# Four graph layers in one kernel: small weights as planned steps, and less of the second group's layer 0 ahead of a branch

## The chip, the cores and the metric

The kernel runs on one core of one Trainium2 chip. The metric is device time in microseconds (us), the median over runs of the whole program.

## The reference

The input is `x`, 128 graphs of 128 nodes with 128 features in float32, and `adj`, an integer matrix 128x128 for each graph (here ones and zeros, one in sixteen set). Four layers follow one another, each as `x = x + layer(relu(layernorm(x)))`, here cut to what matters:

```python
# layer 0: relation r = 1..7, masks of adj == r, averaged over neighbours
for r in range(1, 8):
    mask = (adj == r)
    agg += (mask / clip(mask.sum(2), 1e-6)) @ h @ rel_weights[r]
out = relu(layernorm(agg + h @ self_w.T + self_b) * ln_gamma + ln_beta)
# layer 1: every pair of nodes, a batch norm over all pairs of all graphs
D = abs(h[:, :, None, :] - h[:, None, :, :])           # pairs
p = D @ W1.T + b1
p = leaky((p - mean(p)) / sqrt(var(p) + eps) * g1 + be1)   # mean over batch and pairs
A = softmax(where(adj > 0, p @ W2.T + b2, NEG))
y = leaky(batchnorm(A @ h @ Wg.T + bg))
out = concat([h, y], 2) @ Wt.T + bt
# layer 2: graph attention with 4 heads; layer 3: with one head, elu at the end
```

## The kernel before, in words

The 128 graphs are worked on in 32 groups of four (`G`, `NG`). The program has three long stages. The first does layer 0 and the pair products of layer 1 with their statistics; the second reads the products back, applies the batch norm and the softmax of layer 1; the third does layers 2 and 3. This case concerns the beginning of the first.

**The search and the branch.** Relations 2 to 7 are rare, so the kernel first looks whether `adj` has any entry above 1. `part(c)` loads one of 16 pieces of `adj` (512 KB each, `PARTS`) and `highest(c)` reduces it, on DVE for an even `c` and on ACT for an odd one. `flagged` puts the answer into `flag`. A branch (`tc.If`, L646) reads it on every engine. If relations above 1 occur, a general path computes their share for each group and writes it to `AGG[g]` in DRAM. If not, as here, the other path only writes `selfb`, the broadcast bias, into the whole of `AGG` (L695, two transfers out of the tensors `rest`).

**Layer 0 of a group.** `chain(g)` makes the steps of one group: `load` (x and adj, L428 and L429), `agg` (read of `AGG[g]`, L432), the layer norm's moments on DVE (`mv`) and roots on POOL (`rs`), the mask and the degree, the normed `hn` on ACT, transposes, the products `ph` and `po` on PE, then the second half: `o` (sum with agg, L489), its moments `mvo` and roots `rso`, `oc`, `on`, `end`, the store of x (`x`, L535), the moments and roots for layer 1 (`mvx`, `rsx`) and `h1`, layer 1's input, in two halves. The first `AHEAD` groups are done ahead of the branch with `selfb` in place of `agg`; when the general path is taken, it does them again. Before, `AHEAD` is 2, so groups 0 and 1 are done whole ahead of the branch, and group 2 is only loaded.

**Layer 1's pairs.** For each graph there are four tiles of pairs (`NT`). `difference` (d, L312) subtracts, on DVE for even tiles and on POOL for odd ones; `absolute` is on ACT (L360); `products` on PE (hp, L322 and L325) into two PSUM buffers; `evacuate` copies the product on ACT to a `z` tile of SBUF (L336), one of ten in a ring on the right side of the memory (`held_z`, `FETCHED`); `statistics` is on DVE (L350, L351); and `kept` stores two tiles at a time to DRAM (L343, steps `out0` and `out`). The ring's pool is opened after the branch; the pools of the search and of the branch were closed by then.

**Order.** Each of these is a step with an engine, an estimated cost, the steps that it waits for, and a rank. `_ordered` walks through time, takes at each point the earliest step that can start (the lowest rank among equals), and so writes one program order; each engine executes its steps in that order. There are two such plans, one ahead of the branch and one after it. The plan's costs never touch the hardware: they only set the order. A step on SP is taken to land 3.0 us after its issue (`LANDING`).

**Small weights.** 30 small transfers on SP's queue (biases, norms and weight matrices that later stages use) are written at the head of the second plan, outside of it (`col`, `load`, L198 and L205, and L751 to L766). On the chip 18 of them were issued ahead of the branch and 12 after it, as the trace shows.

Of the kernel before, what the change touches and what calls it, by code (L numbers as in the profile page):

```python
# [9 lines left out]
F32 = mybir.dt.float32  # L10
I32 = mybir.dt.int32
# [6 lines left out]
P = 128  # L18
# [11 lines left out]
ROW = P + 2 * KH  # L30
ON_POOL = {1, 3}
BY_MAX = 0
AHEAD = 2
PARTS = 16
FETCHED = 10
NT = KH // KC
KEPT = 5
# [1 line left out]

ONE, TWO = 4, 2  # L40
PERIOD, FIRST, HOP, LANDING = 12, 5, 0.2, 3.0
HOP1 = 0.4
TINY = 2.0 ** -100
BUFS = {"y": 6, "x": 12, "off": 10, "st": 8, "mv2": 3, "rs2": 3, "nb2": 3, "h": 7, "hT2": 3, "v2": 3, "wr2": 7,
# [4 lines left out]
def _bcast(src, n):  # L49

    return bass.AP(tensor=src.tensor, offset=src.offset, ap=[[0, P], [1, n]])
# [63 lines left out]
def _ordered(steps, limits, hop):  # L115

    named = {s[0]: s for s in steps}
    free, done = dict.fromkeys(("SP", "Pool", "ACT", "DVE", "PE"), 0.0), {}  # L120
    left = {tag: [0.0] * n for tag, n in limits.items()}
    waits = {s[0]: [a for a in s[3] if a in named] for s in steps}
    followers, ready = {}, {e: {} for e in free}
    for name, after in waits.items():
        for a in after:
            followers.setdefault(a, []).append(name)
    missing = {name: len(after) for name, after in waits.items()}

    def released(name):
        engine = named[name][1]  # L130
        ready[engine][name] = max([0.0] + [done[a] + hop * (named[a][1] != engine) for a in waits[name]])

    for name, n in missing.items():
        if n == 0:
            released(name)
    plan = []
    while len(plan) < len(steps):
        best = None
        for engine, names in ready.items():
            could = []  # L140
            for name, since in names.items():
                takes = named[name][4]
                if all(left[tag] for tag in takes):
                    could.append((max([free[engine], since] + [min(left[tag]) for tag in takes]),
                                  named[name][6], name))
            if could:
                first = min(could)[0]
                one = min((c for c in could if c[0] == first), key=lambda c: c[1])
                if best is None or first < best[0]:
                    best = one  # L150
        start, _, name = best
        _, engine, cost, _, takes, gives, _, work = named[name]
        del ready[engine][name]
        free[engine] = start + cost
        done[name] = start + cost + (LANDING if engine == "SP" else 0)
        for tag in takes:
            left[tag].remove(min(left[tag]))
        for tag in gives:
            left[tag].append(start + cost + hop)
        plan.append(work)  # L160
        for f in followers.get(name, ()):
            missing[f] -= 1
            if missing[f] == 0:
                released(f)
    return plan
# [3 lines left out]
def tile_gnn_stack(ctx: ExitStack, tc: tile.TileContext, a: dict, out: bass.AP):  # L169
    nc = tc.nc  # L170
    NB = a["x"].shape[0]
    NG = NB // G

    const = ctx.enter_context(tc.tile_pool(name="const", bufs=1))
# [21 lines left out]
    def load(name, shape, src, pool=const):  # L196
        t = pool.tile(shape, F32, name=name)
        nc.sync.dma_start(t, src)  # L198
        return t

    def col(name, src, n=P, pool=const):

        t = pool.tile([P, 1], F32, name=name)
        for k in range(P // n):
            nc.sync.dma_start(t[k * n:(k + 1) * n, :], src)  # L205
        return t
# [55 lines left out]
    with tc.tile_pool(name="c0", bufs=1) as c0, tc.tile_pool(name="p0", bufs=2) as p0, ExitStack() as ctx0:  # L262
# [2 lines left out]

        sizes = (6, NG - 8)
        rest = [dr.tile([P, n, G, P], F32, tag=f"a{i}", name=f"a{i}") for i, n in enumerate(sizes)]
        AGG = [t[:, i, :, :] for t, n in zip(rest, sizes) for i in range(n)]  # L270
        AGG = [None] * AHEAD + AGG
# [22 lines left out]
        steps = []  # L294

        def step(name, engine, cost, after, rank, work, takes=(), gives=()):
            steps.append((name, engine, cost, after, takes, gives, rank, work))
# [113 lines left out]
        def chain(g, agg=None, again=None):  # L411

            bs = slice(g * G, g * G + G)
            s0 = G * NT * g - 31
            t = {}
            own = lambda *names: [(name, g) for name in names]

            def tile0(name, dtype=F32, **kw):
                pool, tag = p0, name
                if again is not None:  # L420

                    pool, tag = again, {"mask": "mask4", "maskT": "adjT", "o": "adjf"}.get(name, name)
                    kw = dict(bufs=2) if name == "hn" else {}
                t[name] = pool.tile([P, G, P], dtype, tag=tag, name=name, **kw)
                return t[name]

            def loaded():
                nc.sync.dma_start(tile0("x"), a["x"][bs].rearrange("b t c -> t b c"))  # L428
                nc.sync.dma_start(tile0("adj", I32), a["adj"][bs].rearrange("b t s -> t b s"))  # L429

            def added():
                nc.sync.dma_start(tile0("agg"), AGG[g])  # L432
# [66 lines left out]
            def h1(half):  # L499
                if g not in H1:  # L500
                    H1[g] = p0.tile([P, G, P], F32, name="h1", bufs=3)
                for k in (2 * half, 2 * half + 1):
                    nc.scalar.activation(H1[g][:, k, :], t["x"][:, k, :], AF.Relu, bias=t["nb"][:, k:k + 1],  # L503
                                         scale=t["rs"][:, k:k + 1])

            step(("load", g), "SP", 1.2, [("h1", g - 2, 1), ("x", g - 2), ("xp", 2 * g - 5)]
                 + [("part", PARTS - 1)] * (g >= AHEAD), s0 - 2, loaded)
            if agg is None:
                step(("agg", g), "SP", 0.4, own("load"), s0 + 6, added)
            else:  # L510
# [32 lines left out]
        search = ctx0.enter_context(tc.tile_pool(name="sc", bufs=1))  # L543
        found, n_part = {}, P * P // PARTS
# [23 lines left out]
            nc.scalar.copy(selfb, over_group(found["pr"][:, 0, :]))  # L568

        def part(c):  # L570
            found[c] = search.tile([P, n_part], I32, name="part", bufs=PARTS // 2)
            nc.sync.dma_start(found[c], flat[c])

        def highest(c):

            one, by_sum = found.pop(c), c % 2
            if by_sum:
                nc.scalar.activation(one, one, AF.Relu, bias=less_1, accum_out=tops[:, 1, c // 2:c // 2 + 1])
            else:
                nc.vector.tensor_reduce(tops[:, 0, c // 2:c // 2 + 1], one, AX.X, OP.max)  # L580
# [41 lines left out]
        step("on_all", "PE", 0.6, ["small", ("pt", 0)], -98, on_all, takes=("sm",))  # L622
        step("selfb", "ACT", 0.6, ["on_all"], -98, in_group, gives=("sm",))
        for c in range(PARTS):
            step(("part", c), "SP", 20.0 / PARTS, [("top", c - PARTS // 2)], 1 + c / PARTS,
                 lambda c=c: part(c))
            step(("top", c), "ACT" if c % 2 else "DVE", 1.25, [("part", c)], -99, lambda c=c: highest(c))
        step("top", "DVE", 0.4, [("top", c) for c in range(PARTS)], -99, highest_of_all)
        step("ptop", "PE", 0.3, ["top"], -99, one_row, takes=("sm",))
        step("flag", "DVE", 0.4, ["ptop"], -99, flagged, gives=("sm",))  # L630
# [3 lines left out]
        for g in range(AHEAD):  # L634
            chain(g, selfb)

        held = len(steps)
        chain(AHEAD)
        steps[held:], held = steps[held:held + 1], steps[held + 1:]
        with tc.manual_schedule():  # L640
            for work in _ordered(steps, {"sm": 2}, HOP1):
                work()
# [3 lines left out]
        with tc.If(nc.values_load(flag, min_val=0, max_val=1) > 0) as cmp, \  # L646
# [6 lines left out]
            for g in range(NG):  # L653
                x = pr.tile([P, G, P], F32, name="x")
                nc.sync.dma_start(x, a["x"][g * G:g * G + G].rearrange("b t c -> t b c"))
                adj = pr.tile([P, G, P], I32, name="adj")
# [3 lines left out]
                hT = pr.tile([P, G, P], F32, name="hT")  # L660
# [5 lines left out]
                for k in range(G):  # L666
                    mask = pr.tile([P, 6, P], F32, name="mask")
# [56 lines left out]
        a2 = const.tile([P, 2, 4], F32, name="a2")  # L724
        nc.gpsimd.memset(a2, 0.0)

        steps += held[1:]
        held[0][-1]()
        for g in range(NG):
            for half in range(2):  # L730
                features(g, half)
            if g > AHEAD:
                chain(g)
        for i in range(NT * NB):
            pairs(i)
        step("fetch", "SP", 0.8, [("hs", NT * NB - 2), ("st", NT * NB - 2 * NT), ("out", NB - G - 1)], NT * NB, first_fetches)
        with tc.manual_schedule():

            b1 = col("b1", a["b1"], 64)
            g1 = col("g1", a["g1"], 64)  # L740
            be1 = col("be1", a["be1"], 64)
            wgT = load("wgT", [P, P], a["WgT"])
            bg = col("bg", a["bg"])
            gg = col("gg", a["gg"])
            beg = col("beg", a["beg"])
            wtxT = load("wtxT", [P, P], a["WtT"][0:P])
            bt = load("bt", [P, P], _bcast(a["bt"], P))

            nc.sync.dma_start(w2z[0:64, 31:32], a["W2"])  # L751
            nc.sync.dma_start(w2z[64:128, 32:33], a["W2"])
            b2 = load("b2", [P, 1], bass.AP(tensor=a["b2"].tensor, offset=a["b2"].offset, ap=[[0, P], [1, 1]]))
            w2x = const.tile([P, P + 8], F32, name="w2x")
            nc.sync.dma_start(w2x[:, 0:P], a["W_2"])
            w3x = const.tile([P, P + 2], F32, name="w3x")
            nc.sync.dma_start(w3x[:, 0:P], a["W_3"])
            b_2 = load("b_2", [P, P], _bcast(a["b_2"], P))
            b_2c = col("b_2c", a["b_2"])
            wtyT = load("wtyT", [P, P], a["WtT"][P:2 * P])  # L760
            a3 = const.tile([P, 2, 1], F32, name="a3")
            for part in range(2):
                for hd in range(4):

                    nc.sync.dma_start(a2[32 * hd:32 * hd + 32, part, hd:hd + 1], a["a_2"][32 * (1 - part):][0:32])
                nc.sync.dma_start(a3[:, part, :], a["a_3"][P * (1 - part):][0:P])  # L766

            for work in _ordered(steps, {"sm": 2}, HOP1):
                work()

# [854 lines left out]
```

## Time and profile before

| | us |
|---|---|
| time before, median of 3 runs | 2777.38 (2776.46 to 2777.83) |
| the profiled execution, its own time | 2781.11 |
| its span | 2779.3 |
| busy over the span: DVE, PE, ACT, POOL | 2472.0, 2457.4, 2388.7, 1724.0 |
| first to last copy of a product (L336) | 70.9 to 1524.5 |
| copies number 16, 128, 192, 256 (from 0) begin at | 123.4, 442.9, 625.4, 807.9 |

The span is that of the profiled execution from its first to its last instruction. A time in a view counts from the span's start. In a list of instructions the columns are start, duration, engine and line, operation, output and inputs, count, and in brackets the idle time just ahead with the event that ended it. "SPq" is SP's own queue: there a duration is the time that issuing takes, not the transfer.

### The profile page before, as it was taken

What the parts mean: (1) busy time and instruction counts of PE and PEld (TensorE: products, weight loads), DVE (VectorE), ACT (ScalarE), POOL (GpSimd) and SP (SyncE); (2) the same over time, 40 slices, a digit from 0 to 9 for tenths busy, and PEclk for the clock granted to TensorE, in tenths of its full rate; (3) what the DMA queues carried; (4) which work ended last, traced back from release to release, by engine and by line L of the source; (5) the groups of instructions that cost most, each with busy time, mean ns of one, the idle gap of its engine ahead of it and who ended that gap; (6) DMA issues with size and microseconds to landing.
All of it is one profiled execution on the core that took longest, in us unless ns stands there. A gap on an engine that the chain in (4) does not pass through costs nothing.

```text
span 2779.3 us, 42065 instructions
## 1 busy us (share of the span) xinstructions
PE 2457.4 (88%) x14521; PEld 1182.0 (43%) x14521; DVE 2472.0 (89%) x4712; ACT 2388.7 (86%) x2837; POOL 1724.0 (62%) x1629
## 2 busy tenths in 40 slices
PE   3899999999999999999998789888888897999896
PEld 2333333333333333333332344444444445777675
DVE  4899999999999999999999688888888887899976
ACT  4899999999999999999998778778778766899985
POOL 5799999999999999999997001111000115565642
PEclk7999999999999999999999899999999999999998
DMA  7455555555555555555543899999999971121110
GB/s 283 171 223 201 212 201 210 210 212 201 208 201 208 211 209 207 208 207 215 206 193 125 330 409 411 410 411 410 409 410 410 409 266 54 46 69 58 58 31 25
DMA packets 195933, 635.66 MB, mean 229 GB/s; under 512 B 32755, under 2 KB 100470, under 8 KB 132214
## 3 DMA queue, kind: packets, MB, share of 16 engines
q1 hardware_dynamic: 195264, 632.62, 58.6%
q8 instruction: 120, 1.97, 0.3%
q14 instruction: 111, 0.91, 0.1%
q10 hardware_dynamic: 438, 0.17, 0.0%
HBM read 328.84 MB, written 303.89 MB: 228 GB/s over the span
## 4 chain that ended last, share of the span: by engine, by line
ACT 33%; PE 22%; DVE 19%; issue 11%; DMA 10%; POOL 3%; SPq 1%; ACTq 0%; DVEq 0%; POOLq 0%
ACT d L360 11%; ACT z L336 11%; PE hp L322 6%; PE ps L871 5%; DMA rows<-sk 4%; DVE d L312 3%; DMA u<-rows 3%; DVE z L914 3%; DMA z<-hp 3%; PE hp L325 2%; ACT h L1229 2%; PE pk L878 2%; PE pv L1345 2%; ACT o L462 1%; ACT h L503 1%
## 5 line engine op out<-in xcount | busy, mean ns | idle before, releaser
L312 POOL TENSOR_TENSOR d<-xe 128x2048 f32<-128x2048 f32 x256 | 1074.1, 4202 | 67.1 <-PE hp L322 48.9
L322 PE MATMUL hp<-d,w1T 128*64 128x512 f32 x4096 | 999.4, 603 | 119.8 <-ACT z L336 96.8
L360 ACT ACTIVATE d<-d 128x2048 f32<-128x2048 f32 x384 | 734.6, 1935 | 24.7 <-POOL d L312 18.2
L312 DVE TENSOR_TENSOR d<-xe,xp 128x2048 f32<-128x2048 f32 x256 | 579.5, 2264 | 5.8 <-PE hp L322 3.1
L322 PEld LDWEIGHTS hp<-d,w1T 128*64 128x64 f32 x4096 | 286.2, 137 | 640.4 <-issue 466.6
L336 ACT COPY z<-hp 128x1024 f32<-128x1024 f32 x512 | 516.9, 1028 | 47.1 <-PE hp L325 24.4
L962 POOL TENSOR_TENSOR x<-x,bt 128x512 f32<-128x512 f32 x32 | 46.5, 1455 | 672.1 <-DMA x<-x 629.0
L350 DVE BATCH_NORM_STATS2 st<-z 128x6 f32<-128x512 f32 x512 | 349.3, 682 | 42.4 <-ACT z L336 42.1
L351 DVE BATCH_NORM_STATS2 st<-z 128x6 f32<-128x512 f32 (+1 forms) x512 | 329.3, 643 | 0.0
L914 DVE SCALAR_TENSOR_TENSOR z<-z 128x2048 f32<-128x2048 f32 x128 | 296.6, 2317 | 6.5 <-ACT z L896 6.5
L896 ACT ACTIVATE z<-z,bias,scale 128x2048 f32<-128x2048 f32 x128 | 267.1, 2087 | 9.3 <-DVE bias L809 7.7
L325 PE MATMUL hp<-both_t,xw 128*64 128x512 f32 x1024 | 268.3, 596 | 0.0
L900 ACT ACTIVATE zr<-z,bias,scale 128x2048 f32<-128x2048 f32 x128 | 267.3, 2088 | 0.9 <-DMA z<-hp 0.9
L871 PE MATMUL ps<-z,w2z 128*32 128x512 f32 x1024 | 144.7, 638 | 65.1 <-DVE z L914 64.9
L878 PEld LDWEIGHTS pk<-pick,su 128*128 128x128 f32 x1024 | 127.4, 196 | 136.2 <-DVE su L892 94.0
L878 PE MATMUL pk<-pick,su 128*128 128x16 f32 x1024 | 139.9, 269 | 19.9 <-DVE su L892 19.3
L1345 PE MATMUL pv<-wr,e 128*128 128x128 f32 x1024 | 141.7, 285 | 5.8 <-DVE e L1322 4.0
L871 PE MATMUL ps<-z,w2l 128*32 128x512 f32 x1024 | 142.7, 626 | 0.0
L871 PE MATMUL ps<-zr,w2r 128*32 128x512 f32 x1024 | 141.0, 623 | 0.0
L325 PEld LDWEIGHTS hp<-both_t,xw 128*64 128x64 f32 x1024 | 80.7, 138 | 140.7 <-issue 140.7
L1345 PEld LDWEIGHTS pv<-wr,e 128*128 128x128 f32 x1024 | 129.4, 197 | 13.5 <-DVE e L1322 4.1
L1322 DVE SCALAR_TENSOR_TENSOR e<-e,ps 128x512 f32<-128x512 f32 x160 | 106.8, 677 | 25.9 <-ACT ps L1319 25.1
(243 smaller groups left out, 3823.2 us busy)
## 6 DMA issues: line engine op xcount, KB each, us to landing
hp<-z SPq DMA_DIRECT2D x248, 1024.0 KB, 3.9
z<-hp SPq DMA_DIRECT2D x248, 1024.0 KB, 14.2
x<-x SPq DMA_DIRECT2D x118, 256.0 KB, 5.9
u<-rows SPq DMA_DIRECT2D x32, 384.0 KB, 11.6
x<-in_x_dram SPq DMA_DIRECT2D x32, 256.0 KB, 3.1
adj<-in_adj_dram SPq DMA_DIRECT2D x32, 256.0 KB, 3.5
part<-in_adj_dram SPq DMA_DIRECT2D x16, 512.0 KB, 7.6
out_dram<-x SPq DMA_DIRECT2D x32, 256.0 KB, 2.4
```

The source lines that it names most:

```text
L312: eng.tensor_tensor(d, ahead, x[:, None, None, :].to_broadcast([P, 2, KC, P]), OP.max if t == BY_MAX else OP.subtract)
L322: nc.tensor.matmul(hp[64 * hh:64 * hh + 64, c:c + 512], w1T2 if by_max else w1T, d[:, hh, c:c + 512], start=True, stop=not by_max, skip_gr ...
L325: nc.tensor.matmul(hp[64 * hh:64 * hh + 64, c:c + 512], XW[i // NT // 2][:, i // NT % 2, :], both_t.rearrange("p h k i -> p h (k i)")[:, h ...
L336: nc.scalar.copy(half_of(b, t), linear.pop(i))
L350: nc.vector.bn_stats(st[:, 2 * t, :], hs[:, 0:512])
L351: nc.vector.bn_stats(st[:, 2 * t + 1, :], hs[:, 512:1024 - P * last])
L360: nc.scalar.activation(diffs[i], diffs[i], AF.Abs)
L871: nc.tensor.matmul(ps[32 * c:32 * c + 32, :], w[:, w0:w0 + 32], v[:, 512 * c:512 * c + 512], start=j0 == 0, stop=w is w2r, skip_group_chec ...
L878: nc.tensor.matmul(pk[:, kk, 0:16], su[:, kk, :], pick.rearrange("p h j -> p (h j)"), start=True, stop=True)
L900: nc.scalar.activation(zr, z1, AF.Relu, bias=bias1, scale=scale1[:, 0:1])
L914: nc.vector.scalar_tensor_tensor(z0, z0, 0.01, z0, op0=OP.mult, op1=OP.max)
L1345: nc.tensor.matmul(t[pv][:, k % 2, hd, :], t[e][:, hd, :], flat[:, at:at + P], start=True, stop=True)
```

## The change

The group count ahead of the branch goes from 2 to 1. Of group 1 only the steps named in `FRONT` (up to the transposed mask and the first product) stay ahead of the branch; of groups 2 and 3 the loads. Everything else of groups 1 to 3 is added to the second plan. There, `agg` of these groups waits for a step named "bias", which stands for the write of `selfb` with 22 us and runs on an engine of its own in the plan, and the mask and the moments of groups 2 and 3 wait for a product. The write of `selfb` covers 31 groups in place of 30. The tiles `x` get four buffers in place of two, `adj` three. The search's pieces get six buffers (`HELD`) in place of eight; their landing in the plan is 5.5 us, and the reductions have rank -6 in place of -99. The 30 small transfers become steps on SP, one after each second batch's store from batch 8 on.

```diff
-AHEAD = 2
-PARTS = 16
+AHEAD = 1
+FRONT = {"load", "mask", "mv", "deg", "rs", "most", "per", "hn", "share", "pt", "hT", "pm", "maskT", "ph", "hw", "m8",
+         "sd", "nb"}
+PARTS, HELD = 16, 6
...
+SEARCHED, BIAS = 5.5, 22.0
...
-    free, done = dict.fromkeys(("SP", "Pool", "ACT", "DVE", "PE"), 0.0), {}
+    free, done = dict.fromkeys(("SP", "Pool", "ACT", "DVE", "PE", "DMA"), 0.0), {}
...
-        done[name] = start + cost + (LANDING if engine == "SP" else 0)
+        done[name] = start + cost + (0 if engine != "SP" else SEARCHED if name[0] == "part" else LANDING)
...
-        sizes = (6, NG - 8)
+        sizes = (7, NG - 8)
...
-                nc.sync.dma_start(tile0("x"), a["x"][bs].rearrange("b t c -> t b c"))
-                nc.sync.dma_start(tile0("adj", I32), a["adj"][bs].rearrange("b t s -> t b s"))
+                nc.sync.dma_start(tile0("x", bufs=4), a["x"][bs].rearrange("b t c -> t b c"))
+                nc.sync.dma_start(tile0("adj", I32, bufs=3), a["adj"][bs].rearrange("b t s -> t b s"))
...
-            step(("load", g), "SP", 1.2, [("h1", g - 2, 1), ("x", g - 2), ("xp", 2 * g - 5)]
-                 + [("part", PARTS - 1)] * (g >= AHEAD), s0 - 2, loaded)
+            step(("load", g), "SP", 1.2, [("h1", g - 2, 1), ("x", g - 2), ("xp", 2 * g - 5)] * (g > 3)
+                 + [("part", PARTS - 1)] * (g > AHEAD), s0 - 2, loaded)
...
-            found[c] = search.tile([P, n_part], I32, name="part", bufs=PARTS // 2)
+            found[c] = search.tile([P, n_part], I32, name="part", bufs=HELD)
...
-            step(("part", c), "SP", 20.0 / PARTS, [("top", c - PARTS // 2)], 1 + c / PARTS,
+            step(("part", c), "SP", 21.3 / PARTS, [("top", c - HELD)], 1 + c / PARTS,
                  lambda c=c: part(c))
-            step(("top", c), "ACT" if c % 2 else "DVE", 1.25, [("part", c)], -99, lambda c=c: highest(c))
+            step(("top", c), "ACT" if c % 2 else "DVE", 1.35, [("part", c)], -6, lambda c=c: highest(c))
...
-        held = len(steps)
-        chain(AHEAD)
-        steps[held:], held = steps[held:held + 1], steps[held + 1:]
+        held = []
+        for g in range(AHEAD, 4):
+            n = len(steps)
+            chain(g)
+            early_names = FRONT if g == AHEAD else {"load"}
+            held += [one for one in steps[n:] if one[0][0] not in early_names]
+            steps[n:] = [one for one in steps[n:] if one[0][0] in early_names]
...
-        steps += held[1:]
-        held[0][-1]()
+        step("bias", "DMA", BIAS, [], -99, lambda: None)
+        for name, engine, cost, after, takes, gives, rank, work in held:
+            after = after + ["bias"] * (name[0] == "agg") + [("hp", 12 * name[1] - 22)] * (name[0] in ("mask", "mv"))
+            step(name, engine, cost, after, rank, work, takes, gives)
...
-            if g > AHEAD:
+            if g > 3:
                 chain(g)
...
+        for n, (dst, src) in enumerate(later):
+            step(("const", n), "SP", 1.2, [("out", 8 + 2 * n)], NT * (8 + 2 * n) + 2,
+                 lambda dst=dst, src=src: nc.sync.dma_start(dst, src))
         with tc.manual_schedule():
-
-            b1 = col("b1", a["b1"], 64)
-            g1 = col("g1", a["g1"], 64)
...
```

More of the change, by code (lines that the diff above doesn't have):

```diff
@@ L736, in tile_gnn_stack @@
         step("fetch", "SP", 0.8, [("hs", NT * NB - 2), ("st", NT * NB - 2 * NT), ("out", NB - G - 1)], NT * NB, first_fetches)
-        with tc.manual_schedule():
-            b1 = col("b1", a["b1"], 64)
-            g1 = col("g1", a["g1"], 64)
[L741 to L766, printed above, removed]
@@ new lines, in tile_gnn_stack, with in_const, column @@
+        later = []
+        def in_const(name, *parts, n=P, shape=None):
+            t = const.tile(shape or [P, n], F32, name=name)
+            later.extend((place(t), src) for place, src in parts)
+            return t
+        def column(name, src, n=P):
+            return in_const(name, *[(lambda t, k=k: t[k * n:(k + 1) * n, :], src) for k in range(P // n)], n=1)
+        whole = lambda t: t
+        b1 = column("b1", a["b1"], 64)
+        g1 = column("g1", a["g1"], 64)
+        be1 = column("be1", a["be1"], 64)
@@ new lines, in tile_gnn_stack @@
+        wgT = in_const("wgT", (whole, a["WgT"]))
+        bg = column("bg", a["bg"])
+        gg = column("gg", a["gg"])
+        beg = column("beg", a["beg"])
+        wtxT = in_const("wtxT", (whole, a["WtT"][0:P]))
+        bt = in_const("bt", (whole, _bcast(a["bt"], P)))
+        later += [(w2z[0:64, 31:32], a["W2"]), (w2z[64:128, 32:33], a["W2"])]
+        b2 = in_const("b2", (whole, bass.AP(tensor=a["b2"].tensor, offset=a["b2"].offset, ap=[[0, P], [1, 1]])), n=1)
+        w2x = in_const("w2x", (lambda t: t[:, 0:P], a["W_2"]), n=P + 8)
@@ new lines, in tile_gnn_stack @@
+        w3x = in_const("w3x", (lambda t: t[:, 0:P], a["W_3"]), n=P + 2)
+        b_2 = in_const("b_2", (whole, _bcast(a["b_2"], P)))
+        b_2c = column("b_2c", a["b_2"])
+        wtyT = in_const("wtyT", (whole, a["WtT"][P:2 * P]))
+        a3 = in_const("a3", *[(lambda t, k=k: t[:, k, :], a["a_3"][P * (1 - k):][0:P]) for k in range(2)], shape=[P, 2, 1])
+        later += [(a2[32 * hd:32 * hd + 32, part, hd:hd + 1], a["a_2"][32 * (1 - part):][0:32])
+                  for part in range(2) for hd in range(4)]
```

## The prediction

> **What bounds the kernel now.** I read the busy table by stages first, then SP's queue around the branch, then what ACT and DVE waited for behind it. Five stretches (columns: busy microseconds and instruction count of PE, weight load, DVE, ACT, POOL, then TensorE clock, DMA share, GB/s):
>
> ```profile
> 0.00:44.90 44.90, 12.91 (x71) 10.45 (x71) 26.46 (x76) 23.77 (x48) 22.57 (x46) 0.88 0.74 261
> 44.90:70.90 26.00, 10.26 (x36) 4.59 (x36) 6.23 (x11) 5.01 (x7) 16.12 (x10) 0.63 0.86 315
> 70.90:123.40 52.50, 45.93 (x208) 18.17 (x208) 40.69 (x62) 43.12 (x44) 36.88 (x22) 0.90 0.41 160
> 123.40:1525.00 1401.60, 1301.66 (x6223) 499.59 (x6222) 1356.23 (x2297) 1330.19 (x1425) 1312.13 (x770) 1.00 0.53 204
> 1525.00:2779.00 1254.00, 1086.68 (x7986) 649.22 (x7986) 1042.39 (x2267) 986.63 (x1316) 336.31 (x783) 0.95 0.66 256
> ```
>
> From 123.4 to 1525 us DVE is busy 1356.23/1401.60 = 96.8%, ACT 94.9%, POOL 93.6%: time there can only be saved by removing work. The first 123.4 us are loose, and there the change acts. The order of events, from the branch line's own records, SP's queue, and the first waits behind it:
>
> ```profile
> L646 ACTq COMPARE_BRANCH  x1: 50/50/50, 41.5 to 41.5; - x1
> L646 SPq COMPARE_BRANCH  x1: 50/50/50, 44.3 to 44.3; - x1
> ```
>
> ```profile
> 43.81 0.45 SPq L198 DMA_DIRECT2D b<-in_b_dram  x1
> 48.08 1.30 SPq L695 DMA_DIRECT2D a<-selfb  x2
> 49.86 12.45 SPq L205 DMA_DIRECT2D b_2c<-in_b_dram  x1
> 62.37 1.23 SPq L198 DMA_DIRECT2D wtyT<-in_WtT_dram  x1
> 63.64 7.67 SPq L765 DMA_DIRECT2D a<-in_a_dram  x4
> ...
> 74.22 0.40 SPq L428 DMA_DIRECT2D x<-in_x_dram  x1
> ```
>
> ```profile
> 70.90 1.01 ACT L336 COPY z<-hp 128x1024 f32<-128x1024 f32 x1 [14.83 <-DMA a<-in_a_dram]
> ```
>
> ```profile
> 76.97 0.87 DVE L439 BATCH_NORM_STATS2 lnst<-x 128x6 f32<-128x128 f32 x4 [24.04 <-DMA x<-in_x_dram]
> ```
>
> Read so: SP comes to the branch last (44.3), because 18 of the 30 small weight loads stand ahead of it on its queue, from 22.48 us on. Then the fill of `rest` with `selfb` (L695, 30 groups of 256 KB = 7.86 MB) goes out at 48.08. The traffic of the 16 DMA engines stops between 70.0 and 70.5 us, and the first copy of a product out of PSUM (`z`, L336) begins at 70.90. The view names the DMA of `a2` (its tile is called `a`) as that copy's last releaser, but it is preceded by five semaphore waits on ACT at 70.5 to 70.8, and nothing but the end of the fill coincides with them. I take it that the ring of `z` lies where the branch's pools lay and cannot be written until the branch's transfers are done. The other 12 small loads then keep SP to 74.2, so group 3's `x` lands only at about 77, and DVE, which is in order, stands in front of it for 24.04 us, 6.07 of them after the first copy.
>
> **What the Trainium skill says.** "Runtime: NRT & Kernel Launch", Instruction fetch mechanics: a taken branch whose target is outside the fetched pages stalls for a fetch. The trace agrees: TensorE's compare-and-branch took 3.8 us, and SP needed 48.08-44.3 = 3.8 us to its next issue. This price stays. "Perfetto Trace Analysis", Identifying the Most-Contended Engine: for Vector, Scalar and GPSIMD the occupancy is a fair measure of distance from the limit; I use it for the stretch at 96.8%. "DMA: Bandwidth & Descriptors", Two DMAs through the same engine are not ordered: only the completion semaphore orders a read behind a write. So group 1's new read of `AGG[1]` must wait for the first part of the fill; no operation of before shows this wait.
>
> **The change, part by part.**
>
> *Branch earlier.* Three things are ahead of it now: the search, group 0's whole chain, the front half of group 1. The flag was ready at 32.03+0.14 = 32.17 us, behind parts that landed at DMA speed (the last ACT part started at 28.41), and the DMA bytes ahead of it don't grow. Group 0's h1 ended at 39.1 and group 1's at 42.63; group 1's second half goes, and the searches now rank behind group 0's steps. From its rows group 0's chain needs: moments to 4.8, roots to 8.1, table load and hn to 11.1, pt, hT, ph, hw to about 15, po to 17, then o to mvo 2, roots 2, oc 1.65, on and end 2.1, mvx 1.2, roots 2, h1 1.65, in all 29.6, and some 3 to 5 us for searches of 1.2 us that stand in between. SP has 16 parts, 2 zero writes, 4 loads and one store left, and waits for the flag and that store. I take its branch at **34.5** (bounds 33 and 38) against 44.3: 9.8 us earlier. Six `part` buffers in place of eight are the risk: SP already waited 6.0 us for ACT and 1.7 for DVE to free them, though the DMA engines were full. I take nothing for it, as six buffers are 7.7 us of transfer and part-to-landing plus search was 7.6+1.2 with a queue of eight; without that cover it is 1 to 4 us.
>
> *A longer fill.* 31 groups, 8.13 MB in place of 7.86: 0.27 MB at 385 GB/s is 0.7 us. So the first copy comes at 70.9-9.8+0.7 = **61.8**, 9.1 earlier.
>
> *Loads ahead.* `x` and `adj` of groups 2 and 3 are read before the branch (1 MB, about 2.6 us of DMA, beside the search's last steps). DVE's 6.07 us in front of `x` go; so does a part of the other idle time before 140 us, in which it was idle 12 us since the first copy. What is late next is the fifth to eighth difference, restarting from a cold TensorE (16 matmuls took 5.11 us at 72 against 3.65 at 101; "TensorE: Matmul & The Clock Gate", Part 1, says that the clock falls to half after an idle window; the trace has 0.50 from 62 to 74). I take 7 of the 12 (bounds 3 and 11).
>
> *Work put into the bound stretch.* Group 1's second half on DVE: o 0.68, moments 1.15, on 0.69+0.69, end 0.69, moments 1.15, together 5.05. Group 2's mask and moments now wait for the third product: 1.14+0.69 = 1.83 of DVE that used to be done at 45 to 48 us, in the dead time. 6.88/0.968 = 7.1. On POOL: two roots of 1.95, a mask of 1.50 and one more root of 1.95 = 7.35/0.936 = 7.9. ACT: 3.3 us. Overlapped, I charge **7.3** (bounds 5 and 9).
>
> *The small loads.* 30 issues move behind stores of the first stage. SP spends under 1.3 us on each there; its stores wait for `z` copies, and ten `z` buffers cover a delay of that size. If that cover failed, 30 times 1 us would be 30 us, but the DMA share of 0.53 in this stretch speaks against it. The first reader is the end of the stage, far behind store 66. Nothing.
>
> *`AGG[1]`.* On SP it stands behind three product stores; o(1) waits on DVE with statistics and differences queued behind. The plan gives it 22 us and 3 for landing, and ACT's copies are late by about as much, so the read should be issued near 76 and land (4.2 us in the issue table) near 80, as DVE reaches it. Group 1's first difference is wanted 16 products after the first, at 61.8+16x2.85-6 = 101; 20 us suffice when its steps rank first. 0 (bounds 0 and 5).
>
> Sum: -9.1 -7 +7.3 = **-8.8 us**. The profiled execution took 2781.11 for a span of 2779.3, 3.7 above the median of 2777.38. I take the difference off the median: **2768.6**.
>
> **Rivals.** (a) *The search becomes the wait.* With six buffers and searches ranked behind the chains, ACT, which has about 23 us of work in the 24 before the flag, frees the parts late and the branch moves to 38 or 39. The gain is 4 to 5 us, 2773: within what can be told apart. For it: SP's waits on buffers; against: only DMA speed set the end of the search.
> (b) *Another rhythm, the slower side.* The plan's order is fixed by its start. Before, copy 128 begins at 442.9, 192 at 625.4, 256 at 807.9: exactly 182.5 us for each four groups, some 7.75 times. A plan that starts otherwise may settle into another pattern. 0.6% more, 1.1 us in each, eats the gain; from 1.9 us on (184.4) it is slower by 0.2%; at 185 the sum is -8.8+19 = +10, 2788. For it: no engine is quite full and the first 16 copies after 211.3 took 48.7 us, not 45.6. Against it: costs and dependencies of the steady groups are the same, so the old pattern is the likeliest. The same door opens the other way, to 2758.
> (c) *The change doesn't do what it says:* the first copy waits for something else than the fill, or SP still meets the branch late. Then only the 7 us of DVE and the 7.3 of added work remain: 2777.7, no change.
>
> **How the numbers follow.** Forecast 0.48 (nearly all of it faster), (a) 0.14, (b) 0.22 slower or even and 0.08 faster, (c) 0.08. About 0.2%, 5.6 us, is what a measurement of this kernel can tell from no change. Faster by more than that: 0.44 of the forecast, 0.08 of (b), 0.04 of (a), 0.56. Slower: 0.19 of (b) and 0.02 of a late `AGG[1]`, 0.21. Same: 0.23. Range: the bounds of the forecast's terms give 2761 to 2776; reaching into both sides of (b), to the 2788 worked out there, makes it 2757 to 2788.
>
> **What would show it.** Right: SP's branch near 34.5, the fill (1792 and 6144 KB) issued near 38.3, first copy at 61 to 63, no DVE wait for `x`, no small load between branch and first copy, 182.5 us from copy 128 to 192, and copy 192 near 616.6. A flag after 36 is (a); another time between copies 128 and 192 is (b); a first copy that does not follow the fill's end is (c).

## The result and the profile after

| | before | after |
|---|---|---|
| median of 18 runs each, us | 2776.12 (2772.47 to 2783.38) | 2771.95 (2767.46 to 2778.69) |
| ratio of after to before | | 0.9987, 95% interval 0.998 to 0.9994 |
| profiled execution, own time / span, us | 2781.11 / 2779.3 | 2768.47 / 2766.7 |
| flag ready | 32.2 | 35.5 |
| SP at the branch | 44.3 | 36.9 |
| fill of `rest` issued | 48.08 | 39.72 |
| first copy of a product | 70.9 | 63.6 |
| copies 8, 16, 64, 128 (from 0) begin | 100.7, 123.4, 260.0, 442.9 | 86.1, 116.2, 255.2, 436.9 |
| last copy of the first stage | 1524.5 | 1518.5 |

The kernel is faster by 0.13%, with an interval from 0.06% to 0.2%: 1.7 to 5.6 us. The forecast of -8.8 was about twice the 4.2 us between the medians. The change touches nothing behind the first stage, so the steps are judged by the times of the copies. In them the lead over before is 7.3 us at the first copy, 14.5 at copy 8, 13.3 at copy 14, 7.2 at copy 16, and 6.0 at the last. What follows the last copy took between 1248 and 1255 us in the profiles of this study, in no order by kernel. That scatter can account for the difference between 6.0 us in the stage and 4.2 in the medians; this is argued and not shown.

The times of the copies come from one profiled execution of each kernel. How far they can be trusted is seen on the five experiments that leave the order behind copy 16 as it is in after (`x1`, `x4`, `x6`, `x11`, `x12`): their distance to after changes by less than 1 us from copy 16 to the last copy. Smaller differences are not read here.

Stretches of after with about the same borders as in before (branch past, first copy, copy 16, last copy), and the columns of the prediction's table:

```profile
0.00:41.60 41.60, 12.88 (x56) 10.04 (x56) 21.42 (x56) 20.85 (x40) 20.25 (x39) 0.81 0.83 288
41.60:63.60 22.00, 11.00 (x52) 6.94 (x52) 6.86 (x3) 4.84 (x6) 15.96 (x7) 0.73 0.97 361
63.60:116.20 52.60, 44.83 (x202) 17.11 (x204) 46.37 (x93) 45.64 (x52) 40.79 (x31) 0.91 0.47 180
116.20:1518.50 1402.30, 1302.49 (x6228) 501.64 (x6224) 1354.93 (x2294) 1329.17 (x1423) 1309.99 (x769) 1.00 0.54 203
```

The stretch from copy 16 to the last copy is what it was (1402.3 us against 1401.6). The third has the same length as before (52.6 against 52.5), but DVE is busy 46.37 in it instead of 40.69: part of the dead time is gone, and work stands in its place. The branch, SP's queue and the first waits behind it in after:

```profile
L653 ACTq COMPARE_BRANCH  x1: 50/50/50, 36.7 to 36.7; - x1
...
L653 SPq COMPARE_BRANCH  x1: 50/50/50, 36.9 to 36.9; - x1
```

```profile
33.22 1.58 SPq L606 DMA_DIRECT2D rows<-zero  x2
39.72 1.34 SPq L702 DMA_DIRECT2D a<-selfb  x2
67.42 5.02 SPq L346 DMA_DIRECT2D hp<-z  x2
72.49 1.39 SPq L435 DMA_DIRECT2D agg<-a  x2
```

```profile
63.63 1.01 ACT L339 COPY z<-hp 128x1024 f32<-128x1024 f32 x1 [11.96 <-issue]
```

```profile
64.67 0.69 DVE L353 BATCH_NORM_STATS2 st<-z 128x6 f32<-128x512 f32 x1 [11.85 <-ACT z L339]
65.28 0.68 DVE L354 BATCH_NORM_STATS2 st<-z 128x6 f32<-128x512 f32 x1
65.88 0.85 DVE L442 BATCH_NORM_STATS2 lnst<-x 128x6 f32<-128x128 f32 x4
```

No small load is left between the fill and the first store, and DVE's 24.04 us in front of `x` are gone: its moments follow the statistics without a wait. But all engines reach the branch within 0.3 us of one another: they wait for the flag. And the first copy still follows the end of the fill. ACT's queue stood in a wait of 14.2 us ahead of it, and the transfers ended between 62.5 and 63.0 us (the last two columns are the busy share of the DMA engines and GB/s):

```profile
L339 ACTq EVENT_SEMAPHORE  x4: 38/38/14216, 49.1 to 63.6; - x4
```

```profile
62.00:62.50 0.50, 0.00 (x0) 0.00 (x0) 0.00 (x0) 0.00 (x0) 0.00 (x0) 0.50 0.50 184
62.50:63.00 0.50, 0.00 (x0) 0.00 (x0) 0.00 (x0) 0.00 (x0) 0.00 (x0) 0.50 0.06 25
63.00:63.50 0.50, 0.00 (x0) 0.00 (x0) 0.00 (x0) 0.00 (x0) 0.00 (x0) 0.50 0.00 0
```

### The profile page after: what moved, and what is told of

It is laid out like the page before. It is cut to its first block, busy times and chain, and to the rows that moved or that the text cites. A ratio compares the mean times of both kernels' runs of the same rounds, so it can differ in the third digit from the quotient of the medians.

```text
span 2766.7 us, 42019 instructions
## 1 busy us (share of the span) xinstructions
PE 2450.3 (89%) x14521; PEld 1181.3 (43%) x14521; DVE 2470.4 (89%) x4712; ACT 2386.6 (86%) x2837; POOL 1717.5 (62%) x1629
## 4 chain that ended last, share of the span: by engine, by line
ACT 34%; PE 22%; DVE 18%; issue 11%; DMA 10%; POOL 3%; SPq 0%; ACTq 0%; POOLq 0%; DVEq 0%
ACT d L363 12%; ACT z L339 11%; PE hp L325 6%; PE ps L883 5%; DMA rows<-sk 4%; DVE d L315 3%; DVE z L926 3%; DMA u<-rows 3%; DMA z<-hp 3%; PE hp L328 2%; ACT h L1241 2%; PE pk L890 2%; ACT hn L465 2%; ACT o L465 2%; ACT h L506 1%
## 5 line engine op out<-in xcount | busy, mean ns | idle before, releaser
L1357 PEld LDWEIGHTS pv<-wr,e 128*128 128x128 f32 x1024 | 126.7, 194 | 13.3 <-DVE e L1334 4.1
## 6 DMA issues: line engine op xcount, KB each, us to landing
z<-hp SPq DMA_DIRECT2D x248, 1024.0 KB, 14.2
```

## The experiments

The gain has three candidates (SP freed of small loads, group 1's second half taken from ahead of the branch, x loaded early), and two things could take it back (the search, the moved work). One inference of the prediction, that the first copy waits for the fill, carries the largest term. Each expectation names a theory A and one or more rivals. A ratio below is the time over that of before, with its 95% interval. Four kernels (`x4`, `x7`, `x8`, `x12`) ran once only; of them the stage is read, not the time.

**Does the first copy wait for the fill?** The ten `z` tiles are put into two pools of five. The first five then lie on bytes that neither the search's pool nor the branch's ever used; the program order of every engine stays.

```diff
-        ring = early_ring.enter_context(tc.tile_pool(name="ring", bufs=1, side="right"))
+        rings = [early_ring.enter_context(tc.tile_pool(name=f"ring{n}", bufs=1, side="right")) for n in range(2)]
+        turns_z = itertools.count()
...
-            return ring.tile([P, NT // 2 * KC * P], F32, tag="z", bufs=FETCHED, name="z")
+            return rings[next(turns_z) // 5 % 2].tile([P, NT // 2 * KC * P], F32, tag="z", bufs=5, name="z")
```

> The kernel after, with the ten z tiles in two pools of five, the first five on bytes that neither the search nor the branch used; program order of all engines unchanged. Theory A (the first copy waits for the fill of rest because the ring lies on released pools): the first copy comes when its product is ready, at 49.5 to 51.5 us in place of 63.6; copy 8 moves by about as much (86.1 to 73-75), the last copy of the stage from 1518.5 to about 1506, the time by -10 to -13 us against after. Rival B (the first copy waits for something else that ends with the fill): 63.6 stays, and the time. Rival C (the copy is freed, but group 1's read of AGG or its second half then stops the pairs): copy 8 near 74, but copy 16 still near 110 and the time only 3 to 6 us down.

First copy at 52.5, copy 8 at 73.5, copy 16 at 106.6, last copy 1508.1. Time 2763.3, ratio to before 0.9947 (0.9933 to 0.9961). ACT in that kernel from 48 us on, and its engines and DMA from 52 us on:

```profile
48.94 3.70 ACT L363 ACTIVATE d<-d 128x2048 f32<-128x2048 f32 x2
52.54 1.00 ACT L339 COPY z<-hp 128x1024 f32<-128x1024 f32 x1
53.43 1.92 ACT L363 ACTIVATE d<-d 128x2048 f32<-128x2048 f32 x1
```

```profile
52.00:56.00 4.00, 3.75 (x18) 1.00 (x14) 4.00 (x11) 4.00 (x4) 3.64 (x4) 1.00 1.04 391
56.00:60.00 4.00, 3.60 (x18) 1.58 (x20) 3.75 (x5) 2.79 (x4) 4.00 (x3) 1.00 1.03 389
```

The copy carries no bracket: it follows ACT's own work, while the transfers, the fill above all, still move 389 to 391 GB/s beside it. Theory A holds and rival B falls, though the copy came 1 us later than theory A had it (the fill itself went out at 41.4, not 39.7). Rival C falls with the last copy: of the 11.1 us at the first copy, 10.4 are left there.

The program built from each kernel says why. In after the tile of the first copy lies on bytes of the search's pieces and of the general path's tiles, and the copy waits until all eight semaphores that count transfers stand where the general path would leave them. The other path tops these counts up, and the fill's own two increments are part of the sum. So the copy waits for the fill although the fill uses none of these bytes. With two pools the first copy waits for its product alone.

**The small loads alone**, on the kernel before:

> The kernel before, with one part of the change alone: the 30 small loads as steps of the first stage's plan. SP then comes to the branch with ACT, near 42.6, not at 44.3: fill near 46.5, first copy near 69.2 in place of 70.9; group 3's x is issued directly behind the fill, so DVE's wait for it ends before the first copy. Theory A: copy 8 at 92 to 94 in place of 100.7, last copy 5 to 8 us earlier than 1524.5, time as after or 1 to 2 us above it. Rival (SP is held by the read of AGG behind the fill, and x with it): copy 8 at 97 or later, and the time within 2 us of before.

First copy 67.5, copy 8 at 90.5, last copy 1514.7. Time 2768.01, ratio 0.9965 (0.9952 to 0.9979): 9.8 us in the stage, more than the whole change has. SP passes its branch at 40.0 and issues the fill at 43.92; ACT's branch comes only at 41.4. Group 3's x goes out directly behind the fill:

```profile
43.92 1.33 SPq L695 DMA_DIRECT2D a<-selfb  x2
45.80 12.75 SPq L428 DMA_DIRECT2D x<-in_x_dram  x1
```

```profile
68.26 0.87 DVE L439 BATCH_NORM_STATS2 lnst<-x 128x6 f32<-128x128 f32 x4 [17.06 <-DMA x<-in_x_dram]
```

DVE is freed 0.8 us after the first copy, not 6.07 us. Between first and last copy DVE's busy time is what it was (1396.7 against 1396.5 us) and its idle time 50.5 against 57.1. So 3.4 us come from the earlier first copy, and most of the rest from that wait, which fell from 6.07 us behind the first copy to 0.8. The gain was above what theory A expected.

**What the other parts do, then.** Group 1 whole ahead of the branch, everything else as in after (`AHEAD` 2, only loads early):

> The kernel after, but with groups 0 and 1 both done whole ahead of the branch, as before (AHEAD 2, 30 groups filled); groups 2 and 3 loaded ahead, small loads as steps. Theory A (the moved second half is paid back in the full stretch): branch near 41, fill issued near 45, first copy near 67.5, no gap between copies 15 and 16, copy 64 within 2 us of after's 255.2, time within 3 us of after. Rival (the shorter front is what gained): first copy near 67.5 and the lead never made up, last copy near 1522, time 4 us above after, equal to before.

First copy 71.1, copies 15 and 16 at 110.6 and 115.1, last copy 1519.6; time 2774.99, ratio 0.9992 (0.9984 to 1.0001). The first copy is 3.6 us later than expected and 7.4 later than in after, and still the last one is within 1.1 us of after's: what the longer front loses is saved behind it, as theory A said of the moved half. The gap between copies 15 and 16 that theory A had ruled out is 4.5 us, but copy 15 came early: from copy 14 to copy 16 this kernel took 6.3 us, before 6.9 and after 13.0. The flag came only at 42.4. This kernel was not a clean one: as the condition `g > AHEAD` stood, group 2's load went out at 4.0 us, ahead of the search's pieces, so the group's half and the search are mixed in it. It pointed at the search, so that was tried next. Eight buffers (`HELD` 8), and, apart from that, the reductions at their old rank (-99 in place of -6):

> The kernel after, with eight buffers for the search's pieces (HELD 8) in place of six. Theory A (six buffers made SP wait for DVE's reductions and delayed the flag from 32.2 to 35.5): last piece issued near 22 in place of 25.8, flag near 33, first copy near 61.3. Rival (the order of the reductions on DVE and ACT, behind group 0's chain, sets the flag): flag within 0.7 us of 35.5, first copy within 0.7 of 63.6.

> The kernel after with the reductions of the search at rank -99 alone; six buffers and the landing time stay. Theory A (the rank delays the flag, not the buffers): last piece issued by 23, flag at 31 to 33, first copy 60 to 61.5, last copy 1514 to 1516.5. Rival (with six buffers the rank does not help, both are needed): last piece at 24.5 or later, flag at 34 or later, last copy above 1517.

Eight buffers: last piece issued at 22.4, but flag at 35.0 and last copy 1519.3. All pieces had landed by 29.1, but DVE came to its last one only at 32.35, behind group 0's second half. Old rank: last piece issued at 26.1 and landed at 30.4, flag 35.3, last copy 1518.7. Each alone changes nothing that can be read. Both, with the plan's old costs for the pieces:

```diff
-PARTS, HELD = 16, 6
+PARTS, HELD = 16, 8
-SEARCHED, BIAS = 5.5, 22.0
+SEARCHED, BIAS = 3.0, 22.0
-            step(("part", c), "SP", 21.3 / PARTS, [("top", c - HELD)], 1 + c / PARTS,
+            step(("part", c), "SP", 20.0 / PARTS, [("top", c - HELD)], 1 + c / PARTS,
-            step(("top", c), "ACT" if c % 2 else "DVE", 1.35, [("part", c)], -6, lambda c=c: highest(c))
+            step(("top", c), "ACT" if c % 2 else "DVE", 1.25, [("part", c)], -99, lambda c=c: highest(c))
```

> The kernel after with the search as before (rank -99, eight buffers, its old costs), and nothing else changed: one ring of z. Theory A (the change is three parts: small loads -9.8 us, search ranked behind group 0's chain +3.6, group 1's second half and the loads about 0): branch of SP near 34 and of ACT near 37.5, fill near 37, first copy near 60.5, last copy 1514 to 1516, time 2767 to 2769.5, as the small loads alone. Rival (the search part is worth nothing when the fill holds the copy): last copy within 1.5 us of 1518.5, time within 2 us of 2772.

Last piece at 21.2, flag 31.4, SP's branch 34.1, fill at 37.15, first copy 60.7, last copy 1516.8, 0.8 us above what was expected. Time 2767.65, ratio 0.9968 (0.9955 to 0.998). What SP waited for up to 40 us, first in after and then here (columns: total, times, longest):

```profile
SPq L575 <- DVE tops L583: 8.6, 5, 5.0
...
SPq L575 <- ACT part L581: 3.2, 3, 2.5
```

```profile
SPq L575 <- ACT part L581: 5.9, 4, 2.2
...
SPq L575 <- DVE tops L583: 1.8, 1, 1.8
```

In after the reductions on DVE hold the pieces. Why they come late stands in DVE's own order:

```profile
12.04 1.22 DVE L583 TENSOR_REDUCE tops<-part 128x1 f32<-128x1024 int32 x1 [1.64 <-DMA part<-in_adj_dram]
...
14.19 2.29 DVE L615 TENSOR_TENSOR both_t<-turns,ident 128x2048 f32<-128x2048 f32 x1
18.68 0.18 DVE L520 RECIPROCAL deg<-deg 128x4 f32<-128x4 f32 x1 [2.20 <-POOL deg L459]
18.77 2.31 DVE L583 TENSOR_REDUCE tops<-part 128x1 f32<-128x1024 int32 x2
```

From the end of one reduction at 13.26 to the next at 18.77 DVE does other things, 2.20 us of it waiting for POOL, and with six buffers SP runs out. The change's new search as a whole (buffers, rank and costs) costs 3.0 us at the first copy and 1.7 at the last. Buffers and rank together with the costs left as they are in after were not run, so what the costs add is open.

**The gap at copy 16.** In after ACT goes from copy 15 to copy 16 like this, 7.3 us from start to start, where before it took 0.9 us:

```profile
108.92 1.01 ACT L339 COPY z<-hp 128x1024 f32<-128x1024 f32 x1
...
110.95 0.28 ACT L405 ACTIVATE xw<-xp 128x128 f32<-128x128 f32 x1 [0.25 <-PE xp L401]
111.12 3.70 ACT L363 ACTIVATE d<-d 128x2048 f32<-128x2048 f32 x2
116.24 1.02 ACT L339 COPY z<-hp 128x1024 f32<-128x1024 f32 x1 [1.42 <-PE hp L328]
```

Copy 16 is group 1's first. Its `h1` ran at 100.83, on ACT, and the differences could only start then. With the plan's allowance for the fill at 8 us (`BIAS`), the second half stands earlier in the order:

> The kernel after with the plan's allowance for the fill at 8 us, not 22, so that group 1's read of AGG and its second half stand earlier in the order. Theory A (the 7.3 us between copies 15 and 16 are group 1 coming late in the order): gap between copies 15 and 16 under 4 us, copy 16 at 110 to 113 in place of 116.2, last copy 3 to 5 us earlier than 1518.5. Rival (the gap is mere work that must be done there, group 1's 5 us on DVE): copy 16 earlier, but the last copy within 1.5 us of 1518.5.

Gap 3.0 us, copy 16 at 111.4, last copy 1515.7, 2.8 us earlier than after: between the two expectations. From copy 14 to copy 16 it took 5.7 us, less than the 6.9 of before and far less than the 13.0 of after, while copies 0 to 14 took 1.7 us more than in after. So most of the loss there was lateness in the order. Copy 64 came at 247.9, 7.3 us earlier than in after. But between copies 64 and 128 this kernel took 185.7 us and after 181.8: the changed plan lost 3.9 us far behind the place at which it was aimed. Which steps lost them stays open.

**Can more be kept?** Loads as steps and two pools, on the kernel before:

> The kernel before with two parts: small loads as steps, and z tiles in two pools; group 3's x still follows the fill on SP's queue. Theory A (the load ahead of the fill matters only once the copy is freed): first copy near 52, then DVE stands in front of x until about 68, copy 8 at 86 to 90 against 90.5 without the two pools, last copy within 3 us of 1514.7. Rival (the freed copy alone carries the gain): copy 8 below 82, last copy below 1506.

First copy 56.5, copy 4 only at 80.3, copy 8 at 91.3, last copy 1513.7; its one run took 2769.03. The first copy came 4.5 us later than theory A had it and copy 8 missed its range by 1.3 us, but the last copy is where theory A had it: the freed copy brings 1.1 us here against the small loads alone, because DVE still stands in front of group 3's x:

```profile
69.03 0.87 DVE L439 BATCH_NORM_STATS2 lnst<-x 128x6 f32<-128x128 f32 x4 [16.86 <-DMA x<-in_x_dram]
```

So the freed copy needs the early loads. `x9_all_kept_2` below adds to this kernel little else than these (and, with them, the later masks and moments of groups 2 and 3), and its last copy comes 9.3 us earlier, at 1504.3. What the early loads bring without the freed copy was not run alone. With all of it (two pools, old search), group 1 in part or whole ahead:

> The kernel after with z tiles in two pools and the search as before (rank -99, eight buffers, its old costs); group 1's second half stays behind the branch. Theory A (flag then near 32, but group 0's chain sets the branch at 35 to 37): fill 39 to 41, first copy 50.5 to 52.5, last copy 1506 to 1508, no more than 2 us better than with two pools alone. Rival (the search order alone lost 3.3 us): branch near 33.5, last copy near 1504.

> Groups 0 and 1 whole ahead of the branch and the search as before (rank -99, eight buffers, its old costs), groups 2 and 3 loaded ahead, small loads as steps, z tiles in two pools. Theory A (three things gain: small loads off SP, x of group 3 ahead of the fill, first copy freed from the fill; moving group 1's second half and ranking the search lower only cost): SP's branch near 40, ACT's near 41.5, first copy near 52, last copy 1500 to 1503, time 2753 to 2757. Rival (the front is too long with group 1 in it; the shorter front of after is worth as much as it costs): branch at 44 or later and last copy near 1508, as with the two pools alone.

> As x5_all_kept, with one oversight mended: there group 2's load stood ahead of the search's pieces (at 3.6 us), because only groups above AHEAD waited for the last piece; here it comes behind them. Theory A (keeping group 1 whole ahead is worth the 7 us of work that after puts into the full stretch): branch near 41.5, first copy near 52, last copy 1500 to 1503. Rival (a front that ends 5 us later costs as much as it saves): branch 44 or later, last copy at 1504.5 or later, no better than x6_search_first.

`x6_search_first`: fill 37.1, first copy 49.7, last copy 1504.5, time 2759.04, ratio 0.9935 (0.9921 to 0.9949). Its rival held at the last copy: the search part is worth 3.6 us at the last copy against the two pools alone. `x5_all_kept` again had group 2's load ahead of the pieces and came to 1511.2 and 2762.17 (0.9948, 0.9936 to 0.996). Mended, `x9_all_kept_2`: fill 41.3, first copy 55.9, last copy 1504.3, time 2757.21, ratio 0.9937 (0.9923 to 0.995). ACT's branch was near 41.5 as theory A said (SP's at 38.3), the first copy 4 us later than theory A had it, and the end as the rival said: a front that is 4.2 us longer at the fill against work that is saved later, and nothing between them. At copy 16 it was 3.1 us ahead of `x6_search_first` (99.5 against 102.6), and lost that by copy 128. By the ratios both beat before by about 18 us and after by about 14.

> As x6_search_first, with the plan's allowance for the fill at 15 us, not 22. With the copy freed, the plan's clock and the chip's run nearly together: the fill ends near 60, 24 us after the branch, and the read should be wanted there. Theory A (group 1 comes late in the order): gap between copies 15 and 16 falls from 8.7 to 3-6 us, last copy 2 to 4 us below 1504.5. Rival (the read itself, behind the fill, sets group 1's start): copy 16 within 1.5 us of 102.6 and last copy within 1.5 of 1504.5.

On `x6_search_first`, the allowance at 15 us gave a gap of 3.1 us, and the last copy came at 1509.0; time 2762.31 (0.9941, 0.9928 to 0.9955). The gap fell as theory A said, but the last copy rose by 4.5 us, which neither expectation allowed. Copies 4 to 12 took 32.3 us instead of 23.1, yet that was made good: copy 64 came at 241.1 in both kernels. As in `x7_early_bias`, the loss lies between copies 64 and 128: 185.7 us against 181.8. So an order that is right at copy 16 can cost more behind it; which steps paid stays open.

## Why the prediction was right and wrong

- *The chain from SP to fill to first copy* was right, and the inference that the copy waits for the fill is shown by the two pools. The size was off: 61.8 predicted, 63.6 measured. The step that failed is "I take nothing for it", on the six buffers, together with searches that rank behind group 0's steps: the flag came at 35.5, not 32.2. Eight buffers alone left it at 35.0 and the old rank alone at 35.3, so either of the two holds it there. Part of that was given back: SP came to its branch at 36.9, 2.4 us later than predicted, and went from there to the fill in 2.8 us, not 3.8. Fill to copy was 23.9 us where 22.8 + 0.7 had been taken.
- *Rival (a)* is what happened in kind, at 2773 by its sum: all engines waited for the flag. But I had named ACT as the engine that frees the pieces late, and it was DVE above all (SP waited 8.6 us for DVE and 3.2 for ACT).
- *Loads ahead*, -7, looked right as far as copy 8: the lead grew from 7.3 to 14.5 us. But the small loads' leaving alone, without the early loads, let it grow by 6.8 (from 3.4 to 10.2), so the growth is no proof of what I credited to the early loads.
- *Work put into the stretch*, +7.3: DVE's busy time between first and last copy went from 1396.5 to 1401.3, +4.8; one more difference (2.3 us) was done ahead of the first copy, which is about what is missing. Its idle time fell by 3.5, not 7. Together the stretch from first to last copy got 1.3 us longer, where -7+7.3 said 0.3. That these two terms agree so well in their sum is luck: they missed by 3.5 and 2.5 us in opposite directions.
- *AGG[1] costs nothing* failed, though not at the read, which was issued at 72.5; o(1) began at 81.20 without a wait, as argued. The error lies further on: "20 us suffice when its steps rank first". The first difference of group 1 came late, and the way from copy 14 to copy 16 took 13.0 us, not 6.9: there 6.1 us of the lead went.
- *The small loads cost nothing in the first stage*: no cost is seen; with them as steps and nothing else changed, the stage got 9.8 us shorter.
- *Rival (b)*: copies 128 and 192 lie 182.5 us apart, as before. The old rhythm stayed from there on.
- Summed: -7.3 and +1.3 make the -6.0 at the last copy, against -9.1 and +0.3. That a fall clear of 0.2% was the likeliest case was too much; the measured one is below it.

The three parts, by the last copy and taken in this order: small loads -9.8 (shown alone), group 1's second half with the early loads and old search +2.1 (1516.8 against 1514.7), the new search +1.7. In the second part the half and the loads are not told apart. The small loads' leaving, which the prediction never priced by itself, carried the gain. Moving group 1's half, with the loads, brought SP's branch from 40.0 to 34.1 and the first copy 6.8 us forward, and gave nothing at the end.

## What to carry to other kernels

When a buffer's first use comes after a branch or a phase change, ask which released pool its bytes belong to. Here the first copy waited for every transfer counted up to the end of the branch, one among them that never touched its bytes, and placing the first buffers on untouched bytes cost no memory and brought 10.4 us at the end of the stage. Work that is taken from a loose stretch into a full one has to be paid there: here the first copy came 6.8 us earlier for it and the last one 2.1 us later. Look first for what ends the loose stretch, here a queue of small loads. In a plan written by costs, a change that is right at its own place can lose behind it: follow the lead over the whole stage, not only at the gap that was to be closed.

## What the runs showed of the hardware

At this branch SP did not wait for the other engines. With the old search in after, the fill went out at 37.15 and ACT's branch came only at 37.5. For the small loads alone I had expected SP at the branch together with ACT, near 42.6; SP passed it at 40.0 and ACT at 41.4. The flag's read took 0.46 to 0.54 us in before, where at most two engines read it at a time, and 1.03 to 1.12 us in after, where all five read it from 35.5 on. That is not a fixed price: all five together took 0.72 to 0.82 us in `x7_early_bias` and 1.42 to 1.53 in `x1_two_rings`, and DVE by itself took up to 0.77. The first two copies lay 2.7 us apart in after, when the transfers had ended (63.63 and 66.35), and 2.7 us in `x1_two_rings` beside transfers of 389 to 391 GB/s (52.54 and 55.24).
